# Maximum over keys by VectorE's block transposes, sums of squares by ScalarE's accumulator

## The chip, the core and the metric

The kernel runs on one core of a Trainium2 chip. A core has five engines, each with its own queue that is executed in order: TensorE (PE, matmuls and transposes, with weight loads that overlap), VectorE (DVE), ScalarE (ACT), GpSimd (POOL) and SyncE (SP), which here issues transfers. They wait for each other by semaphores. PE writes only to PSUM, a memory of eight banks of 128 partitions by 512 floats; POOL works on SBUF here.

The metric is the device time of one execution in microseconds, as the median of several. Lower is better.

## What is computed

The reference is a decoder of two layers on 4 sequences of 256 tokens of width 256: self attention, cross attention with a context of 1601 tokens, feed forward, recurrence, a second cross attention, and a mixture of experts. The change lies in the second cross attention, cut here to what matters:

```python
q = (draft_hidden @ Wq.T).reshape(bsz, draft_len, 16, 128)
q = _rms_norm(q, q_norm_w)            # w * x * rsqrt(mean(x*x) + 1e-6)
kv_in = jnp.concatenate([context_hidden, draft_hidden], axis=1)
k = (kv_in @ Wk.T).reshape(bsz, total_len, 4, 128)
v = (kv_in @ Wv.T).reshape(bsz, total_len, 4, 128)
k = _rms_norm(k, k_norm_w)
q = _rope(q, draft_position_ids)
k = _rope(k, full_position_ids)
k = jnp.repeat(k, 4, axis=1); v = jnp.repeat(v, 4, axis=1)
scores = q k^T * SCALE
probs = jax.nn.softmax(scores, axis=-1)
return (probs @ v) @ Wo.T
```

Here the "draft" is the token stream (256 a sequence), so a query sees 256 + 1601 = 1857 keys. There are 16 query heads and 4 key heads; four query heads share a key head.

## The kernel before

The program has two parts. In the first, up to about 540 us, the earlier stages of all sequences run, with preparation of the context's values and some keys in the gaps. The second part is the second cross attention of all sequences, with the experts of finished sequences mixed in; after the last pair the last experts follow.

**Pairs.** The attention is cut into 32 pairs: 4 sequences x 4 key heads x 2, a pair being two query heads of one key head, 512 query columns. The 1857 keys are 15 blocks of 128 (the last has 65 rows); keys lie on the partitions, queries along the free dimension. A pair is run in 8 steps of two blocks. `score` (L1349) multiplies a block of transposed keys with the pair's queries into a PSUM bank `bsc`; ACT copies it to SBUF with the key's norm as a scale (L1350, tile `s`), and DVE folds it with the same scale into a running maximum `acc` over blocks (L1352, L1354). `acc` is 128 x 512: for each query, 128 maxima over 15 keys each.

**Maximum.** `maximum` (L1356) makes of it one number for each query, the same in all partitions. PE transposes the four 128 x 128 squares of `acc` into `tm` (L1361), DVE reduces each row (L1363, `mq`, 128 x 4), and PE transposes the four columns of `mq`, each broadcast along 128, into the bank `bc` (L1367): there each partition holds the 512 maxima.

**Softmax and values.** `exponential` subtracts `bc` from a step's scores (DVE, L1371), takes the exponential (ACT, L1374) and adds the two blocks to a sum on POOL (L1377, L1386). `weigh` (L1395) multiplies values by the exponentials into the bank `po`. `finish` copies `po` (L1401), gets the sums of the queries by `ts` (PE, L1409) and a block transpose (DVE, L1415), and applies the output weights (PE, L1425, then DVE, L1429).

**Queries and keys.** `prep_q` (32 calls, each 128 tokens of four query heads) multiplies tokens with weights into `pq` (L1227); `prep_kv` makes up to four key blocks, two to a bank `pk` (L1278), or takes keys that were kept earlier from memory (`rawk`, sequence 3). Both call `rotate`: ACT squares the bank's numbers into the tile `squares` (L1177), DVE multiplies by the cosine and sine tables (L1178, L1179, tiles `rope` and `ropu`). Then `factor`: POOL adds the halves (L1184), DVE reduces the squares to `ss`, four numbers a partition (L1186), and POOL takes the power -1/2 (L1187, `rnq` for queries, `kn` for keys). The tile `squares` has a 129th column that holds the epsilon. For queries `normed` scales by `rnq` on ACT (L1191), then PE transposes (L1239, `tpq`) and ACT copies to `qT` (L1240); keys are transposed (L1289, `tpk`) and copied to `kT` (L1291).

**PSUM.** In the second part six banks are a ring (`p1`) for all short uses, one is `bc` and one `po`.

**Order.** Step s emits the exponentials of step s - 10, the scores of step s, the pieces put at place 2s, the values of step s - 11, and the pieces put at place 2s + 1. `put` gives a piece its place; with `bank=True` it moves to the next place that no other such piece has. For pair n with last step e, the two pieces of `maximum` stand at 2e + 2 (or the next free place) and 2e + 5. When the program is built, the instructions of all engines are put into a final order for each queue from this emission, so neighbours can change places. `squares` is one tile for all calls.

Of the kernel before, what the change touches and what calls it, by code (L numbers as in the profile page):

```python
# [10 lines left out]
F32 = mybir.dt.float32  # L11
# [4 lines left out]
AF = mybir.ActivationFunctionType  # L16
ALU = mybir.AluOpType
AX = mybir.AxisListType
PSUM = bass.MemoryType.PSUM

P = 128
# [8 lines left out]
NKV, REP, HD1 = 4, 4, 128  # L30
# [86 lines left out]
def decoder_kernel(ctx: ExitStack, tc: tile.TileContext, at, t, out):  # L117
    nc = tc.nc
    V, A, G, T = nc.vector, nc.scalar, nc.gpsimd, nc.tensor
# [6 lines left out]
    fr = ctx.enter_context(tc.tile_pool(name="fr", bufs=1))  # L126
# [11 lines left out]
    def p1(name):  # L138

        ring[0] += 1  # L140
        if psb and ring[0] % 3 == 0:
            return psb[0].tile([P, 512], F32, tag="one", name=name, bufs=2)
        return psa.tile([P, 512], F32, tag="one", name=name, bufs=4)
# [8 lines left out]
    def bank(tag, name):  # L152

        return psb[0].tile([P, 512], F32, tag=tag, name=name) if psb else p1(name)
# [14 lines left out]
    def db(name):  # L169

        return wk.tile([P, 1024], F32, tag="db", name=name, bufs=NDB)

    def sm(shape, tag, name, bufs=2, dt=F32):
        return small.tile(shape, dt, tag=tag, name=name, bufs=bufs)
# [30 lines left out]
    def cc(name):  # L205
        o, n = at[name]
        return cst[:, o : o + n]

    ident = cc("ident")
# [98 lines left out]
    def w512(tag, name):  # L308
        return fr.tile([P, 512], F32, tag=tag, name=name, bufs=2 if tag == "ropu" else NROPE)
# [855 lines left out]
        bt[b]["yT"] = yT.rearrange("p (c t) -> p c t", c=2)  # L1165


    squares = fr.tile([P, 4, HD1 + 1], F32, tag="sqr", name="squares")
    V.memset(squares[:, :, HD1 : HD1 + 1], HD1 * 1e-6)

    def rope_tiles(nm):
        return squares, *(w512(t, f"{t}{nm}").rearrange("p (h d) -> p h d", h=4) for t in ("rope", "ropu"))

    def rotate(src, ctab, stab, sq, r, u):


        A.activation(sq[:, :, 0:HD1], src, AF.Square)  # L1177
        V.tensor_mul(r, src, ctab)  # L1178
        V.tensor_mul(u, src, stab)  # L1179

    def factor(sq, r, u, n, nm, rn):

        r4, u4 = (a[:, 0:n, :].rearrange("p n (h d) -> p n h d", h=2) for a in (r, u))
        G.tensor_tensor(r4, r4, u4[:, :, ::-1, :], ALU.add)  # L1184
        ss = sm([P, 4], "ss4", f"ss{nm}", 4)
        V.tensor_reduce(ss[:, 0:n], sq[:, 0:n, :], AX.X, ALU.add)  # L1186
        G.tensor_tensor(rn, ss[:, 0:n], nhalf[:, 0:n], ALU.pow)  # L1187

    def normed(r, rn, n):
# [3 lines left out]
    def tiles(b, g):  # L1193

        if (b, g) not in gt:
            gt[b, g] = {

                "kT": odd("w3", f"kTb{b}{g}") if g % 2 else wk.tile([P, NKEY], F32, tag="kT", name=f"kTb{b}{g}"),
                "v": (
                    odd("w4", f"vb{b}{g}")[:, 0 : NCH * HD1] if g % 2 else wk.tile([P, NCH * HD1], F32, tag="v", name=f"vb{b}{g}")  # L1200
                ).rearrange("p (c d) -> p c d", c=NCH),
                "kn": sm([P, NCH], f"kn{g % 2}", f"kn{b}{g}", 1),
                "wkv": weight(
                    wk.tile([P, 512], F32, tag="wkv", name=f"wkv{b}{g}", bufs=2), "wkv1", 0, D, g * 256, (g + 1) * 256
                ),
            }
            for i in range(4):
                if (b, i) in kept_values:
                    n, w = units(i)
                    r = min(P, w)  # L1210
                    nc.sync.dma_start(
                        out=gt[b, g]["v"][0:r, 4 * i + 2 : 4 * i + 2 + n, :],
                        in_=kept_values[b, i][:, 0:r, g * HD1 : (g + 1) * HD1].rearrange("c p n -> p c n"),
                    )
        return gt[b, g]
# [30 lines left out]
    def prep_kv(b, g, i):  # L1246

        d, e = bt[b], tiles(b, g)
        nm = f"k{b}{g}{i}"
        n = min(4, NCH - 4 * i)  # L1250
        k0 = max(0, 4 * i - 2)
        w = (4 * i + n - 2 - k0) * P
        done = 0
        if b in kept_keys:
            done = n if i else 2
            raw = db(f"raw{nm}")[:, 0 : done * HD1].rearrange("p (c d) -> p c d", c=done)
            nc.sync.dma_start(
                out=raw, in_=kept_keys[b][k0 : k0 + done, :, g * HD1 : (g + 1) * HD1].rearrange("c p n -> p c n")
            )
        else:  # L1260
            cT = db(f"cT{nm}")[:, 0 : 2 * w].rearrange("p (c n) -> p c n", c=2)
            nc.sync.dma_start(out=cT, in_=t["ctxT"][b][:, k0 * P : k0 * P + w].rearrange("(c p) n -> p c n", p=P))
        sq, r, u = rope_tiles(nm)
        if done:
            o = n - done
            ctab, stab = (a[:, 4 * i + o : 4 * i + n, :] for a in d["k"])
            rotate(raw, ctab, stab, *(a[:, o:n, :] for a in (sq, r, u)))
        for h in range(0, n - done, 2):
            m = min(2, n - h)
            pk = p1(f"p{nm}{h}").rearrange("p (c n) -> p c n", c=2)  # L1270
            there = [k >= 2 and (b, (k - 2) // 4) in kept_values for k in range(4 * i + h, 4 * i + h + m)]
            for q in range(m):
                k = 4 * i + h + q
                w = HD1 if there[q] else 2 * HD1
                for c in range(2):
                    o = (k - 2 - k0) * P
                    src = d["yT"][:, c, k * P : (k + 1) * P] if k < 2 else cT[:, c, o : o + P]
                    T.matmul(pk[:, q, 0:w], lhsT=src, rhs=e["wkv"][:, c, 0:w], start=c == 0, stop=c == 1)  # L1278
            ctab, stab = (a[:, 4 * i + h : 4 * i + h + m, :] for a in d["k"])
            rotate(pk[:, 0:m, 0:HD1], ctab, stab, *(a[:, h : h + m, :] for a in (sq, r, u)))  # L1280
            assert len(set(there)) == 1
            if not there[0]:
                A.copy(e["v"][:, 4 * i + h : 4 * i + h + m, :], pk[:, 0:m, HD1:256])

        factor(sq, r, u, n, nm, e["kn"][:, 4 * i : 4 * i + n])
        yield
        tp = p1(f"tp{nm}")
        for q in range(n):
            T.transpose(tp[:, q * P : (q + 1) * P], r[:, q, :], ident)  # L1289
        w = min(512, NKEY - 512 * i)  # L1290
        A.copy(e["kT"][:, 512 * i : 512 * i + w], tp[:, 0:w])  # L1291

    def before_head(b, g):
# [6 lines left out]
        for i in (1, 2, 3):  # L1300
            gen = prep_kv(b, g, i)
            next(gen)
            yield
            if late:
                run(late)
                yield
            late = gen
# [17 lines left out]
    class Pair:  # L1325
# [30 lines left out]
        def maximum(self):  # L1356

            nm, acc = self.nm, self.acc
            tm = p1(f"tm{nm}")
            for i in range(4):  # L1360
                T.transpose(tm[:, i * P : (i + 1) * P], acc[:, i * P : (i + 1) * P], ident)  # L1361
            mq = sm([P, 4], "mq", f"mq{nm}")
            V.tensor_reduce(mq, tm.rearrange("p (i k) -> p i k", i=4), AX.X, ALU.max)  # L1363
            yield
            self.bc = bank("bc", f"bc{nm}")
            for i in range(4):
                T.transpose(self.bc[:, i * P : (i + 1) * P], mq[:, i : i + 1].to_broadcast([P, P]), ident)  # L1367

        def exponential(self, c):
            n, w, s = self.rows[c], self.wide[c], self.s[c]  # L1370
# [77 lines left out]
    def put(place, gen, last=False, bank=False):  # L1448
        while bank and place in taken:
            place += 1  # L1450
        if bank:
            taken.add(place)
        places.setdefault(place, []).append((gen, last))
        return place

    def loader(b, g):
        load_wo(b, g)
        yield

    def tokens(b):  # L1460
        normed_tokens(b)
        yield
        bt[b]["xh"] = bt[b]["centred"]()
        yield
        token_features(b)
        yield

    for n, pair in enumerate(pairs):
        e = NPAIR * n + NPAIR - 1
        gen = pair.maximum()  # L1470
        put(2 * e + 2, gen, bank=True)
        put(2 * e + 5, gen, True)
        e += DW
        gen = pair.finish()
        put(2 * e + 1, gen)
        if not pair.final:
            put(2 * e + 4, gen, bank=True)
        put(2 * e + 7, gen, pair.final, bank=True)
        if not pair.final:
            put(2 * e + 10, gen, True, bank=True)  # L1480
    for k, (b, g) in enumerate(heads):
        base = 32 * (k - 1)
        if k:
            if g == 0:
                gen = angles(b)
                for i in range(9):
                    put(base - 81 + 6 * i, gen, i == 8)
                gen = tokens(b)
                for i, o in enumerate((-8, -6, -3)):
                    put(base + o, gen, i == 2, i == 2)  # L1490
                for o, n in ((-5, "q"), (-3, "q"), (7, "k"), (11, "k")):
                    gen = tables(b, n) if o in (-5, 7) else gen
                    put(base + o, gen, o in (-3, 11))
            for f, when in ((prep_q, QA), (prep_kv, KA)):
                for i, o in enumerate(when):
                    gen = f(b, g, i)
# [4 lines left out]
        gen = loader(b, g)  # L1501
        put(base + 60, gen, True)
    for b in range(B - 1):
        gen = experts(b)
# [81 lines left out]
    gen = experts(B - 1)  # L1586
# [71 lines left out]
```

## Time and profile before

| | us |
|---|---|
| median of 3 runs (1750.13 to 1754.91) | 1750.22 |
| span of the profiled execution | 1749.1 |
| PE busy in 560 to 1690 us (1130 us) | 1112.0 |
| DVE busy there | 902.6 |
| ACT busy there | 682.7 |
| POOL busy there | 751.3 |
| one pair, from one last score to the next (mean of 31) | 37.1 |

How to read the lines further down. The page's first line gives for each engine the busy time, its share of the span and its instructions; the granted clock of PE was 1.00 over 560 to 1690 us. The "chain that ended last" is the sequence of work followed back from the last instruction, at each step to what released it; its shares say which engine the end waited for. A line of a group has line number, engine, operation, tiles, shape and count, then total busy time in us and mean in ns, then the idle time of the engine just ahead of them and what ended it. A line of the chain in order of time has start, length, engine, line, tile and count; a line of the timeline has start, length, engine, line, operation, tiles, shape, count, and the idle time ahead in brackets.

### The profile page before, as it was taken

How to read it: one execution, taken by the hardware profiler on the slowest of the kernel's cores; microseconds unless marked ns; L12 is line 12 of the kernel's file. 1: busy time of each engine (PE TensorE's matmuls, PEld its weight loads, DVE VectorE, ACT ScalarE, POOL GpSimd, SP SyncE). 2: the span in 40 equal slices, each digit the busy share in tenths (PEclk: the TensorE clock that was granted, in tenths of full speed). 3: DMA queues.
4: the chain of work that ended last, by engine and by line, in shares of the span. 5: the costliest groups of instructions: out<-in, count | busy, mean ns of one | idle time of the engine just before them, and what ended most of it. 6: DMA issues, size and time to landing. Idle time of an engine off the chain costs nothing.

```text
span 1749.1 us, 20626 instructions
## 1 busy us (share of the span) xinstructions
PE 1691.1 (97%) x6636; PEld 970.2 (55%) x6636; DVE 1302.7 (74%) x2428; ACT 998.2 (57%) x1741; POOL 877.0 (50%) x719
## 2 busy tenths in 40 slices
PE   7989989999999999999999999999999999999998
PEld 4555668765555454554555555555555555455546
DVE  5662575788658787787878879787877878888776
ACT  2457653555456566566565646656564655656551
POOL 2210023311016667677666656765666777576651
PEclk9999999999999999999999999999999999999999
DMA  6321234213231021111212121120212112011102
GB/s 226 119 95 55 79 98 136 71 57 104 94 115 43 33 89 28 61 35 54 78 38 64 47 76 52 55 83 31 76 52 73 46 45 91 9 56 49 43 0 67
DMA packets 113138, 119.10 MB, mean 68 GB/s; under 512 B 9968, under 2 KB 86660, under 8 KB 113032
## 3 DMA queue, kind: packets, MB, share of 16 engines
q1 hardware_dynamic: 111736, 116.25, 21.4%
q10 hardware_dynamic: 1296, 1.54, 0.3%
q8 instruction: 53, 0.87, 0.2%
q14 instruction: 53, 0.43, 0.1%
HBM read 100.20 MB, written 17.57 MB: 67 GB/s over the span
## 4 chain that ended last, share of the span: by engine, by line
PE 65%; DVE 12%; POOL 9%; ACT 9%; issue 4%; DMA 1%; POOLq 0%; ACTq 0%; DVEq 0%
PE bpo L1395 16%; PE bsc L1349 16%; PE pk L1278 5%; POOL sum L1386 5%; PE mph L1041 2%; PE bpw L1425 2%; PE vah L348 2%; ACT s L1374 2%; ACT s L1350 2%; DVE acc L1354 1%; PE xpo L728 1%; DVE s L1371 1%; PE pq L1227 1%; POOL ropeq L1184 1%; PE sc L564 1%
## 5 line engine op out<-in xcount | busy, mean ns | idle before, releaser
L1386 POOL TENSOR_TENSOR sum<-sum,s 128x512 f32<-128x512 f32 (+1 forms) x411 | 537.5, 1308 | 84.0 <-ACT s L1374 58.9
L1349 PE MATMUL bsc<-qTb,kTb 128*128 128x512 f32 (+1 forms) x960 | 458.4, 597 | 6.6 <-ACT kTb L1291 6.3
L1395 PE MATMUL bpo<-s,vb 128*128 128x512 f32 (+1 forms) x960 | 458.7, 596 | 0.4 <-ACT s L1374 0.4
L1350 ACT ACTIVATE s<-bsc,kn 128x512 f32<-128x512 f32 (+1 forms) x480 | 317.4, 684 | 210.9 <-PE bsc L1349 193.7
L1354 DVE SCALAR_TENSOR_TENSOR acc<-bsc,kn,acc 128x512 f32<-128x512 f32 x448 | 332.4, 742 | 88.0 <-ACT s L1350 75.0
L1371 DVE TENSOR_TENSOR s<-s,bc 128x1024 f32<-128x1024 f32 (+1 forms) x256 | 289.0, 1140 | 14.8 <-PE bc L1367 14.8
L1374 ACT ACTIVATE s<-s 128x1024 f32<-128x1024 f32 (+1 forms) x256 | 256.6, 1006 | 52.0 <-DVE s L1371 50.5
L1349 PEld LDWEIGHTS bsc<-qTb,kTb 128*128 128x128 f32 (+1 forms) x960 | 173.9, 187 | 191.1 <-issue 135.7
L1395 PEld LDWEIGHTS bpo<-s,vb 128*128 128x128 f32 (+1 forms) x960 | 169.7, 190 | 141.5 <-issue 137.4
L1184 POOL TENSOR_TENSOR ropek<-ropek,ropuk 128x512 f32<-128x512 f32 (+1 forms) x64 | 78.3, 1224 | 123.8 <-DVE ropuk L1179 119.4
L1377 POOL TENSOR_TENSOR sum<-s 128x512 f32<-128x512 f32 x32 | 40.9, 1279 | 195.9 <-ACT s L1374 195.9
L1191 ACT ACTIVATE ropeq<-ropeq,rnq 128x128 f32<-128x128 f32 x128 | 41.2, 390 | 109.7 <-POOL rnq L1187 106.0
L348 PE MATMUL vah<-wv,vcT 128*128 128x512 f32 (+1 forms) x156 | 77.9, 636 | 5.6 <-DMA vcT<-in_ctxT 3.6
L1278 PEld LDWEIGHTS pk<-wkv,cTk 128*128 128x128 f32 x624 | 76.3, 192 | 8.3 <-issue 4.8
L1278 PE MATMUL pk<-wkv,cTk 128*128 128x128 f32 x624 | 77.4, 275 | 0.0
L1187 POOL TENSOR_TENSOR kn<-ssk,nhalf 128x4 f32<-128x4 f32 (+1 forms) x64 | 66.2, 1035 | 17.5 <-DVE ssk L1186 17.5
L1425 PEld LDWEIGHTS bpw<-wo,aT 128*128 128x128 f32 x256 | 48.5, 190 | 34.8 <-issue 22.0
L269 POOL TENSOR_TENSOR rsr_xa<-rse_xa,nhalf 128x2 f32<-128x2 f32 x4 | 3.4, 854 | 126.0 <-DVE rse_xa L267 126.0
L1425 PE MATMUL bpw<-wo,aT 128*128 128x256 f32 x256 | 65.6, 379 | 0.3 <-ACT aT L1401 0.3
L1352 DVE TENSOR_SCALAR acc<-bsc,kn 128x512 f32<-128x512 f32 x32 | 24.0, 750 | 56.3 <-ACT s L1350 56.3
L1184 POOL TENSOR_TENSOR ropeq<-ropeq,ropuq 128x512 f32<-128x512 f32 x32 | 43.9, 1371 | 40.2 <-PE bsc L1349 17.8
L351 ACT COPY vst<-vah 128x512 f32<-128x512 f32 (+1 forms) x52 | 30.3, 592 | 58.4 <-PE vah L348 20.6
(505 smaller groups left out, 2584.5 us busy)
## 6 DMA issues: line engine op xcount, KB each, us to landing
v<-vst SPq DMA_DIRECT2D x48, 256.0 KB
vb<-v SPq DMA_DIRECT2D x48, 256.0 KB
cTk<-in_ctxT SPq DMA_DIRECT2D x24, 512.0 KB
wq<-in_wq SPq DMA_DIRECT2D x16, 512.0 KB
wo<-in_wo SPq DMA_DIRECT2D x16, 512.0 KB
wi<-in_wi SPq DMA_DIRECT2D x32, 256.0 KB
vcT<-in_ctxT SPq DMA_DIRECT2D x12, 512.0 KB
xcT<-in_ctxT SPq DMA_DIRECT2D x12, 512.0 KB
```

Of the source, the lines that this page charges most:

```text
L348: T.matmul(pv[0:r, :], lhsT=cT[:, c, k * P : k * P + r], rhs=wv[c], start=c == 0, stop=c == 1)
L1184: G.tensor_tensor(r4, r4, u4[:, :, ::-1, :], ALU.add)
L1187: G.tensor_tensor(rn, ss[:, 0:n], nhalf[:, 0:n], ALU.pow)
L1278: T.matmul(pk[:, q, 0:w], lhsT=src, rhs=e["wkv"][:, c, 0:w], start=c == 0, stop=c == 1)
L1349: T.matmul(pc[0:n, :], lhsT=e["kT"][:, k * P : k * P + n], rhs=q, start=True, stop=True)
L1350: A.activation(s[0:n, i, :], pc[0:n, :], AF.Copy, scale=e["kn"][0:n, k : k + 1])
L1354: V.scalar_tensor_tensor(self.acc[0:n, :], pc[0:n, :], e["kn"][0:n, k : k + 1], self.acc[0:n, :], ALU.mult, ALU.max)
L1371: V.tensor_tensor(s[0:n, 0:w, :], s[0:n, 0:w, :], self.bc[0:n, None, :].to_broadcast([n, w, 512]), ALU.subtract)
L1374: A.activation(s[0:n, 0:w, :], s[0:n, 0:w, :], AF.Exp)
L1386: G.tensor_tensor(self.sum[0:n, :], self.sum[0:n, :], s[0:n, i, :], ALU.add)
L1395: T.matmul(self.po, lhsT=e["v"][0:n, k, :], rhs=self.s[c][0:n, i, :], start=k == 0, stop=k == NCH - 1)
L1425: T.matmul(pw[:, j * 256 : j * 256 + 256], lhsT=aT[:, o : o + P], rhs=e["wo"][:, self.h + h, :], start=True, stop=True)
```

## The change

Two edits, and two places for the pieces of `maximum`.

*Maximum.* DVE transposes `acc` in blocks of 32 x 32 straight into a bank `tr`, so that within each of 4 x 16 blocks keys and queries change places, and reduces over each block's 32 columns to `top`, 128 x 16: for each query, four partial maxima in the four groups of 32 partitions. One PE transpose brings `top` to 16 x 128 (`tm`); DVE reduces over the four groups (`mq`, 16 x 32) and repeats the result four times (`mqf`, 16 x 128); one PE transpose brings this to 128 x 16 (`tq`); and a block transpose by DVE of `tq`, each column repeated 32 times, writes `bc`.

*Sums of squares.* ACT squares each 128 x 128 block by itself and adds up its rows in the instruction's accumulator output, into `ss`; `squares` keeps only the elements, which nobody reads. DVE adds the epsilon to `ss` in place of the reduction.

*Places.* `maximum` has three pieces: at 2e, at 2e + 2 and at 2e + 4, the last two at places free of other pieces that take a bank.

```diff
-    squares = fr.tile([P, 4, HD1 + 1], F32, tag="sqr", name="squares")
-    V.memset(squares[:, :, HD1 : HD1 + 1], HD1 * 1e-6)
+    squares = fr.tile([P, HD1], F32, tag="sqr", name="squares")
...
-    def rotate(src, ctab, stab, sq, r, u):
-        A.activation(sq[:, :, 0:HD1], src, AF.Square)
+    def rotate(src, ctab, stab, ss, r, u):
+        for i in range(ss.shape[1]):
+            A.activation(squares, src[:, i, :], AF.Square, accum_out=ss[:, i : i + 1])
         V.tensor_mul(r, src, ctab)
         V.tensor_mul(u, src, stab)
...
-        ss = sm([P, 4], "ss4", f"ss{nm}", 4)
-        V.tensor_reduce(ss[:, 0:n], sq[:, 0:n, :], AX.X, ALU.add)
+        V.tensor_scalar(ss[:, 0:n], ss[:, 0:n], HD1 * 1e-6, None, ALU.add)
         G.tensor_tensor(rn, ss[:, 0:n], nhalf[:, 0:n], ALU.pow)
...
         def maximum(self):
             nm, acc = self.nm, self.acc
+            tr = p1(f"tr{nm}")
+            V.transpose(tr, acc)
+            top = sm([P, 16], "top", f"top{nm}")
+            V.tensor_reduce(top, tr.rearrange("p (b k) -> p b k", k=32), AX.X, ALU.max)
+            yield
             tm = p1(f"tm{nm}")
-            for i in range(4):
-                T.transpose(tm[:, i * P : (i + 1) * P], acc[:, i * P : (i + 1) * P], ident)
-            mq = sm([P, 4], "mq", f"mq{nm}")
-            V.tensor_reduce(mq, tm.rearrange("p (i k) -> p i k", i=4), AX.X, ALU.max)
-            yield
+            T.transpose(tm[0:16, 0:P], top, ident)
+            mq = sm([16, 32], "mq", f"mq{nm}")
+            V.tensor_reduce(mq, tm[0:16, 0:P].rearrange("b (a i) -> b i a", a=4), AX.X, ALU.max)
+            mf = sm([16, 4, 32], "mqf", f"mqf{nm}")
+            V.tensor_copy(mf, mq[:, None, :].to_broadcast([16, 4, 32]))
+            yield
+            tq = p1(f"tq{nm}")
+            T.transpose(tq[:, 0:16], mf.rearrange("b a i -> b (a i)"), ident[0:16, 0:16])
             self.bc = bank("bc", f"bc{nm}")
-            for i in range(4):
-                T.transpose(self.bc[:, i * P : (i + 1) * P], mq[:, i : i + 1].to_broadcast([P, P]), ident)
+            V.transpose(self.bc.rearrange("p (b k) -> p b k", k=32), tq[:, 0:16, None].to_broadcast([P, 16, 32]))
...
         gen = pair.maximum()
+        put(2 * e, gen)
         put(2 * e + 2, gen, bank=True)
-        put(2 * e + 5, gen, True)
+        put(2 * e + 4, gen, True, bank=True)
```

More of the change, by code (lines that the diff above doesn't have):

```diff
@@ L1165, in token_features, with factor @@
         bt[b]["yT"] = yT.rearrange("p (c t) -> p c t", c=2)
-    squares = fr.tile([P, 4, HD1 + 1], F32, tag="sqr", name="squares")
-    V.memset(squares[:, :, HD1 : HD1 + 1], HD1 * 1e-6)
+    squares = fr.tile([P, HD1], F32, tag="sqr", name="squares")
     def rope_tiles(nm):
-        return squares, *(w512(t, f"{t}{nm}").rearrange("p (h d) -> p h d", h=4) for t in ("rope", "ropu"))
-    def rotate(src, ctab, stab, sq, r, u):
-        A.activation(sq[:, :, 0:HD1], src, AF.Square)
+        ss = sm([P, 4], "ss4", f"ss{nm}", 4)
+        return ss, *(w512(t, f"{t}{nm}").rearrange("p (h d) -> p h d", h=4) for t in ("rope", "ropu"))
+    def rotate(src, ctab, stab, ss, r, u):
+        for i in range(ss.shape[1]):
+            A.activation(squares, src[:, i, :], AF.Square, accum_out=ss[:, i : i + 1])
         V.tensor_mul(r, src, ctab)
         V.tensor_mul(u, src, stab)
-    def factor(sq, r, u, n, nm, rn):
+    def factor(ss, r, u, n, nm, rn):
         r4, u4 = (a[:, 0:n, :].rearrange("p n (h d) -> p n h d", h=2) for a in (r, u))
         G.tensor_tensor(r4, r4, u4[:, :, ::-1, :], ALU.add)
-        ss = sm([P, 4], "ss4", f"ss{nm}", 4)
-        V.tensor_reduce(ss[:, 0:n], sq[:, 0:n, :], AX.X, ALU.add)
+        V.tensor_scalar(ss[:, 0:n], ss[:, 0:n], HD1 * 1e-6, None, ALU.add)
         G.tensor_tensor(rn, ss[:, 0:n], nhalf[:, 0:n], ALU.pow)
@@ L1266, in prep_kv @@
             ctab, stab = (a[:, 4 * i + o : 4 * i + n, :] for a in d["k"])
-            rotate(raw, ctab, stab, *(a[:, o:n, :] for a in (sq, r, u)))
+            rotate(raw, ctab, stab, *(a[:, o:n] for a in (sq, r, u)))
         for h in range(0, n - done, 2):
@@ L1279, in prep_kv @@
             ctab, stab = (a[:, 4 * i + h : 4 * i + h + m, :] for a in d["k"])
-            rotate(pk[:, 0:m, 0:HD1], ctab, stab, *(a[:, h : h + m, :] for a in (sq, r, u)))
+            rotate(pk[:, 0:m, 0:HD1], ctab, stab, *(a[:, h : h + m] for a in (sq, r, u)))
             assert len(set(there)) == 1
```

## The prediction

> **What bounds the kernel now.** I read the page's busy shares first, then the chain that ended last, then the chain in order of time inside the second cross attention, and last the groups of the lines the change touches.
>
> ```profile
> PE 1691.1 (97%) x6636; PEld 970.2 (55%) x6636; DVE 1302.7 (74%) x2428; ACT 998.2 (57%) x1741; POOL 877.0 (50%) x719
> PE 65%; DVE 12%; POOL 9%; ACT 9%; issue 4%; DMA 1%; POOLq 0%; ACTq 0%; DVEq 0%
> ```
>
> TensorE (PE) is busy 97% of the span and carries 65% of the chain. But a busy PE need not work at its pace, so the pace is taken from the chain, which lists matmuls by the distance from one to the next:
>
> ```profile
> 847.70 1.72 PE bsc L1349 x4
> 849.42 1.78 PE pk L1278 x16
> 852.92 0.86 PE bpw L1425 x4
> 865.54 0.44 PE tm L1361 x4
> 872.05 0.44 PE bc L1367 x4
> 905.31 0.79 PE pl L993 x8
> 919.15 0.36 PE ts L1409 x8
> ```
>
> A 512-wide pass costs 1.72/4 = 0.43 us, a 256-wide one 0.215, a pk 0.111, a transpose 0.11, a ts 0.045, a pl 0.10. Between 560 and 1690 us the groups of PE count 1925 passes of 512, 604 of 256, 548 pk, 604 transposes, 240 ts and 24 pl: 828 + 130 + 61 + 66 + 11 + 2 = 1098 us of work in 1130 us. PE is 97% full by pace too. In this stage DVE is busy 77 to 84% of each 100 us, ACT 56 to 64%, POOL 60 to 72% (busy time by stretches).
>
> ```profile
> L1191 ACT ACTIVATE ropeq<-ropeq,rnq 128x128 f32<-128x128 f32 x128 | 41.2, 390 | 109.7 <-POOL rnq L1187 106.0 <-POOL ropeq L1184 3.7
> L1363 DVE TENSOR_REDUCE mq<-tm 128x4 f32<-128x512 f32 x32 | 21.8, 681 | 2.3 <-PE tm L1361 2.2
> L1367 PE MATMUL bc<-cst,mq 128*128 128x128 f32 x128 | 20.0, 280 | 7.2 <-DVE mq L1363 7.2
> L1415 DVE STREAM_TRANSPOSE sq<-ts 128x128 f32<-128x128 f32 x32 | 9.8, 305 | 1.4 <-PE ts L1409 1.4
> L1186 DVE TENSOR_REDUCE ssk<-squares 128x4 f32<-128x516 f32 x48 | 32.5, 676 | 3.8 <-ACT squares L1177 3.8
> L1177 ACT ACTIVATE squares<-pk 128x256 f32<-128x256 f32 x88 | 33.3, 387 | 17.5 <-PE pk L1278 15.7 <-ACT kTb L1291 1.7
> L1177 ACT ACTIVATE squares<-pk 128x128 f32<-128x128 f32 x12 | 3.3, 277 | 0.8
> ```
>
> The 32 missing microseconds of PE come mostly from where ACT, in order, stands 106 us in all (31 times, 3.4 us each) before L1191, for POOL's rnq; keys and scores behind it are late then.
>
> **Part 1, PE.** Per pair eight transposes go and two come. Removed: 32 x 8 x 0.11 = 28.2 us. Added: tm, 128 wide, 0.11; tq, 16 wide, between a ts (0.045) and a transpose (0.11), nearest to pl's 8 columns at 0.10: 32 x 0.21 = 6.7. Net -21.5 us (-23.2 to -21.1). On a PE that is 97% full this counts in full if the others keep up.
>
> **Part 2, DVE, the maximum.** Removed: one reduction, 0.68. Added: two block transposes of 128x512, a 512-wide reduction, a 16x128 reduction and a 16x128 copy. No 128x512 transpose is in the trace. Bounds: 0.305 (the 128x128 one) and 4 x 0.305 = 1.22; I take 0.305 plus what 384 more columns cost a tensor_tensor (0.684 at 512, 0.280 at 128): 0.71. The wide reduction is 0.68 by L1363; the small one 0.28 (0.17 to 0.42, by the 128x16 and 128x256 reductions: 0.16 and 0.41); the copy 0.20 by a 13x128 conversion (0.17 to 0.28). Sum 0.71 + 0.68 + 0.28 + 0.20 + 0.71 = 2.58, so +1.90 a pair, +61 us in all (+30 to +100).
>
> The row first: four PE transposes take 0.44 us of the full engine, and the 128x128 block transpose 0.305 of one that has 20% left. The Trainium skill ("VectorE: DVE Perf Modes", Rules for kernel authors) says the opposite of this edit: a 128x128 transpose belongs on TensorE, DVE does only 32x32 blocks, and chained DVE operations should be few. By the rule the edit is a loss of the +61 us; by the rows it is a gain of 21.5, as DVE is not what fills.
>
> **Part 3, DVE, the sums of squares.** 96 reductions go: 32.5 + 8.7 + 21.7 = 62.9 us. 96 additions on 128x4 come, 0.17 each by the 128x4 tensor_scalar of L267: 16.3. So DVE in all: 61 - 63 + 16 = +14 us (-17 to +54), 1% of the span. At DVE's 12% of the chain: +1.7 us.
>
> **Part 4, ACT.** 148 squares (64.4 us over their six forms) become 368 of 128x128, each with an accumulator output. The plain one takes 0.277. No accumulator output is in the trace. Below: 368 x 0.277 - 64.4 = +37. Above: a second small instruction each, as long as the smallest ACTIVATE of the trace (128x2, 0.204): +113. The nearest row is L1191, a 128x128 with one small second operand, 0.390: 143.5 - 64.4 = +79 us, which I take. It lies in ACT's idle time (40% of the stage); at ACT's 9% of the chain it costs 7 us, nothing if hidden, 79 if the cover is gone. What stands behind a longer square on ACT are the copies s<-bsc that free PSUM banks, and on DVE the product L1178, which waits for the square of the same bank.
>
> The skill ("VectorE: DVE Perf Modes", Two Vector instructions with no wait between them) counts a Vector operation with an accumulator output as two instructions, the operation and a read. It speaks of VectorE; if ACT does likewise, the upper end, +113, is the right one, 3 us more on the path. No run here shows it.
>
> **Part 5, the new waits.** Before, PE's queue held tm, which needs acc, and bc, which needs mq; only a few bc waited, 7.2 us in all.
>
> ```profile
> 858.89 0.75 DVE L1354 SCALAR_TENSOR_TENSOR acc<-bsc,kn,acc 65x512 f32<-65x512 f32 x1 [1.82 <-ACT s L1350]
> 865.38 0.60 PE L1361 MATMUL tm<-cst,acc 128*128 128x128 f32 x4
> ```
>
> Here acc ends at 859.6 and tm starts 5.7 us later. Over all pairs acc ends 1.7 to 4.8 us after the last score's matmul. Now tm needs acc, block transpose and reduction in DVE's queue, and behind tm PE's queue holds bpo and the next pair's bsc. In the order in which the changed program stands, PE has 5 to 8 us of work at the paces above between the last bsc and tm; DVE has, after acc's 1.7 to 2.5, 0.7 to 2.3 us of other work, 0.71, up to 0.7 and 0.68: 3.8 to 6.9. Second pairs of a key head have margin, first pairs none: 16 x 0.25 = 4 us. From tm to tq PE mostly has 2.6 us of work, DVE 0.28 + 0.68 + 0.20 and the latencies: just enough. I take +4 us; bounds -7 (bc's old waits go, none come) and +32 (64 waits of half a microsecond). DVE's wait for bc (14.8 us at L1371) goes, since bc is now its own. Three PSUM banks of the ring instead of one are taken for 1 to 2 us each per pair, within the same bounds.
>
> **Without cost:** additions of places only move pieces within the built order. On SP one load of kept keys (rawk) now stands behind two stores of out; before, they left at 1470.51 and 1470.96, side by side: nothing. POOL keeps its work; rnq now always stands directly behind ropeq, where before 9 of 32 had a sum between, or stood before it, which is at most a gain of 9 x 1.3 us of waiting that is off PE. The last pair: bc was 6.9 us behind the last score's matmul, now about 6.3: nothing.
>
> **Sum.** -21.5 + 1.7 + 7 + 4 = -9 us against the profiled span of 1749.1; the median of the runs, 1750.2, is 1.1 above that span, which I take as what lies around it: 1740.1 + 1.1 = 1741 us.
>
> **Rivals.**
> *All of it arrives.* ACT's and DVE's additions lie in idle time and bc's waits of 7 us go in part: -21.5 - 3: 1726 us. For it: PE is full by pace, ACT 40% idle. Against: POOL, DVE and ACT together hold 30% of the chain, so not every freed microsecond of PE is one of the end.
> *The chain moves to the preparation of the queries.* PE reaches each of the 32 spots at L1191 earlier and waits there: POOL's sum, ropeq and rnq (1.3 + 1.2 + 1.0 us) set the pace. If each takes back 0.65 us, 21 us are gone: 1750 us. For it: the 106 us of ACT waiting. Against: PE has some 14 to 17 us of work between pq and tpq.
> *Slower: DVE stands behind the squares.* L1178 and L1179 are in DVE's queue and wait for four squares where they waited for one. By 0.390 a square: queries 4 x 0.390 - 0.594 = 0.97, x32 = 31 us; keys 2 x 0.390 - 0.387 = 0.39, x88 = 35 us; 66 us in which DVE stands, and acc, which frees the score banks of PE, stands behind. DVE's 903 busy us of these 1130 become 903 + 14 + 66 = 983, 87%. If half reaches PE, -21.5 + 1.7 + 4 + 33 = +17: 1767 us. It decides from a quarter (16 us) on: then the sum is zero. For it: L1178 already waited 25.7 us for the queries' squares. Against: the build's order fills the gap with other work of DVE.
> That the change does not do what it says is ruled out: the changed program has 192 matmuls fewer and 220 ACTIVATEs more.
>
> **Numbers.** Forecast 0.45 (own range 1732 to 1750), all arrives 0.17, back to nothing 0.16, slower 0.22. A measurement of this kernel tells 0.3%, 5 us, from no change, so faster is below 1745. Faster: 0.17 and four fifths of the forecast, 0.54; same: 0.21; slower: 0.25. The range runs from the full arrival, 1725, to short of the slower rival, 1761.
>
> **What would show it.** tm and tq together 32 x 0.21 us of PE, L1395 and L1349 unchanged; DVE's block transposes at 0.7; ACT squares at 0.28 to 0.48 with or without a second instruction behind; idle of PE before tm and tq under 10 us. It is wrong if block transposes take over 1.2 us, if PE stands over 20 us before tm and tq, or if DVE's wait for squares rises above 60 us.

## The result and the profile after

The changed kernel takes 1771.59 us (median of 4 runs, 1770.46 to 1772.84), the kernel before 1751.69 us (4 runs, 1750.13 to 1754.91). The ratio is 1.0113, 95% interval 1.0100 to 1.0125: 20 us slower, where 9 us faster was forecast. The profiled execution spans 1770.8 us.

The page after, its first line and the shares of the chain that ended last:

```profile
PE 1684.8 (95%) x6444; PEld 945.7 (53%) x6444; DVE 1336.5 (75%) x2555; ACT 1055.1 (60%) x2329; POOL 872.6 (49%) x719
PE 59%; ACT 14%; DVE 14%; POOL 7%; issue 5%; DMA 1%; POOLq 0%; ACTq 0%; DVEq 0%; SPq 0%
```

No other engine became full. PE has 192 matmuls less, but its share of the chain fell from 65% to 59%, and ACT's rose from 9% to 14%: PE stands more. Where, the groups after show (busy time and mean, then the idle time of the engine ahead of them):

```profile
L1191 ACT ACTIVATE ropeq<-ropeq,rnq 128x128 f32<-128x128 f32 x128 | 43.8, 392 | 111.4 <-POOL rnq L1187 111.4
L1365 PE MATMUL tm<-cst,top 128*16 128x128 f32 x32 | 8.7, 273 | 9.5 <-DVE top L1362 7.7 <-ACT ropeq L1191 1.9
L1372 PE MATMUL tq<-cst,mqf 16*128 16x16 f32 x32 | 7.2, 227 | 19.1 <-DVE mqf L1369 18.2 <-ACT s L1350 0.9
L1360 DVE STREAM_TRANSPOSE tr<-acc 128x512 f32<-128x512 f32 x32 | 22.8, 713 | 0.1
L1374 DVE STREAM_TRANSPOSE bc<-tq 128x512 f32<-128x512 f32 x32 | 23.0, 719 | 0.8 <-PE tq L1372 0.8
L1186 DVE TENSOR_SCALAR ssk<-ssk 128x4 f32<-128x4 f32 x48 | 22.9, 476 | 3.2 <-ACT squares L1178 3.2
L1178 ACT ACTIVATE squares<-pk 128x128 f32<-128x128 f32 x188 | 52.4, 279 | 30.9 <-PE pk L1278 27.4
L1178 ACT ACTIVATION_READ_ACCUMULATOR squares<-pk 128x1 f32 x188 | 37.7, 201 | 0.0
L1179 DVE TENSOR_TENSOR ropek<-pk,ctabk 128x256 f32<-128x256 f32 x88 | 36.8, 418 | 16.2 <-ACT squares L1178 13.5 <-PE pk L1278 1.7 <-DMA k<-kst 0.4
L1349 PE MATMUL bsc<-qTb,kTb 128*128 128x512 f32 x896 | 430.7, 602 | 14.1 <-ACT kTb L1291 10.2 <-DVE acc L1354 1.9 <-DVE ssq L1186 1.4
```

PE stands 9.5 us before tm and 19.1 us before tq, 28.6 us in all; the prediction called itself wrong from 20 us on. Before, the two groups in these places (tm and bc) had 0.8 and 7.2 us. The last line shows a second place where PE waits: its scores stand 10.2 us for ACT's copy of the transposed keys, `kTb` (6.3 us before).

How such a wait comes about, in the timeline of after, first PE, then DVE (start, length, engine, line, operation; the wait stands in brackets). Of the 32 pairs it is the one with the longest way on DVE from the start of tm to the end of mqf, 6.8 us; the mean is 2.9.

```profile
1075.11 0.28 PE L1365 MATMUL tm<-cst,top 128*16 128x128 f32 x1 [1.15 <-DVE top L1362]
1075.23 1.02 PE L1402 MATMUL bpo<-s,vb 128*128 128x512 f32 x2
1076.09 1.88 PE L1349 MATMUL bsc<-qTb,kTb 128*128 128x512 f32 x4
1077.81 1.02 PE L1402 MATMUL bpo<-s,vb 128*128 128x512 f32 x2
1081.93 0.23 PE L1372 MATMUL tq<-cst,mqf 16*128 16x16 f32 x1 [3.10 <-DVE mqf L1369]
1082.09 1.12 PE L1402 MATMUL bpo<-s,vb 128*128 128x512 f32 x2
```

```profile
1077.59 0.42 DVE L1047 SCALAR_TENSOR_TENSOR it<-it,mph 128x256 f32<-128x256 f32 x1 [2.53 <-ACT it L1046]
1078.75 0.75 DVE L1352 TENSOR_SCALAR acc<-bsc,kn 128x512 f32<-128x512 f32 x1 [0.74 <-ACT s L1350]
1079.41 0.41 DVE L1048 TENSOR_TENSOR it<-it,mph 128x256 f32<-128x256 f32 x1
1079.74 0.74 DVE L1354 SCALAR_TENSOR_TENSOR acc<-bsc,kn,acc 128x512 f32<-128x512 f32 x1
1080.40 0.27 DVE L1367 TENSOR_REDUCE mq<-tm 16x32 f32<-16x128 f32 x1
1080.60 1.14 DVE L1126 SCALAR_TENSOR_TENSOR ang<-sn,ang 128x960 f32<-128x960 f32 x1
1081.67 0.21 DVE L1369 COPY mqf<-mq 16x128 f32<-16x128 f32 x1
```

tm is done at 1075.4. mq needs nothing more, but stands in DVE's queue behind work that waits for ACT (2.53 and 0.74 us), and comes 5.0 us later; between mq and mqf stands another operation, of 1.14 us. PE has 3.4 us of work between tm and tq, so it waits 3.1 us.

### The profile page after: what moved, and what is told of

The parts are those of the page before. It is cut to its first block, busy times and chain, and to the rows that moved or that the text cites. A ratio compares the mean times of both kernels' runs of the same rounds, so it can differ in the third digit from the quotient of the medians.

```text
span 1770.8 us, 20974 instructions
## 1 busy us (share of the span) xinstructions
PE 1684.8 (95%) x6444; PEld 945.7 (53%) x6444; DVE 1336.5 (75%) x2555; ACT 1055.1 (60%) x2329; POOL 872.6 (49%) x719
## 4 chain that ended last, share of the span: by engine, by line
PE 59%; ACT 14%; DVE 14%; POOL 7%; issue 5%; DMA 1%; POOLq 0%; ACTq 0%; DVEq 0%; SPq 0%
PE bpo L1402 15%; PE bsc L1349 15%; PE pk L1278 5%; ACT s L1350 3%; ACT s L1381 3%; PE vah L348 3%; DVE acc L1354 2%; POOL sum L1393 2%; PE mph L1041 2%; ACT ropeq L1191 2%; PE pq L1227 2%; PE bpw L1432 2%; POOL rnq L1187 2%; PE xpo L728 1%; DVE s L1378 1%
## 5 line engine op out<-in xcount | busy, mean ns | idle before, releaser
L1349 PE MATMUL bsc<-qTb,kTb 128*128 128x512 f32 (+1 forms) x960 | 463.2, 601 | 14.1 <-ACT kTb L1291 10.2
L1402 PE MATMUL bpo<-s,vb 128*128 128x512 f32 (+1 forms) x960 | 463.5, 598 | 0.0
L1191 ACT ACTIVATE ropeq<-ropeq,rnq 128x128 f32<-128x128 f32 x128 | 43.8, 392 | 111.4 <-POOL rnq L1187 111.4
L1187 POOL TENSOR_TENSOR kn<-ssk,nhalf 128x4 f32<-128x4 f32 (+1 forms) x64 | 65.1, 1019 | 16.3 <-DVE ssk L1186 13.5
L1178 ACT ACTIVATE squares<-pk 128x128 f32<-128x128 f32 x188 | 52.4, 279 | 30.9 <-PE pk L1278 27.4
```

Of the source, the lines that this page charges most:

```text
L1349: T.matmul(pc[0:n, :], lhsT=e["kT"][:, k * P : k * P + n], rhs=q, start=True, stop=True)
L1402: T.matmul(self.po, lhsT=e["v"][0:n, k, :], rhs=self.s[c][0:n, i, :], start=k == 0, stop=k == NCH - 1)
```

## The experiments

Times are medians; "before" is the kernel before on the same chip. Unless said, kernels start from after. Outside every range that was expected for them fell e3, e5, h1 and h2 by 1 us or less, and f2, f3, g1, g2, g4 and h4 by more (f2 and h4 on the fast side).

| kernel | us | before | ratio, 95% interval |
|---|---|---|---|
| e1_max_only | 1763.07 | 1753.77 | 1.0049 (1.0033 to 1.0065) |
| e2_squares_only | 1752.53 | 1753.77 | 0.9992 (0.9983 to 1.0002) |
| e3_split_only | 1757.14 | 1753.77 | 1.0018 (1.0008 to 1.0027) |
| e5_sq_no_eps | 1743.32 | 1753.77 | 0.9936 (0.9921 to 0.9951) |
| f1_no_copy | 1758.49 | 1753.77 | 1.0036 (1.0023 to 1.0048) |
| f2_late | 1747.75 | 1753.77 | 0.9968 (0.9956 to 0.9979) |
| f3_pe_free | 1756.40 | 1753.77 | 1.0018 (1.0009 to 1.0027) |
| f4_no_eps | 1750.16 | 1753.77 | 0.9978 (0.9969 to 0.9987) |
| g1_eps_reduce | 1776.78 | 1753.01 | 1.0143 (1.0127 to 1.0158) |
| g2_best | 1751.10 | 1753.01 | 0.9993 (0.9983 to 1.0004) |
| g3_max_late | 1748.67 | 1753.01 | 0.9980 (0.9970 to 0.9989) |
| g4_late_pe_kept | 1765.89 | 1753.01 | 1.0079 (1.0064 to 1.0094) |
| h1_power_first | 1757.88 | 1753.63 | 1.0029 (1.0019 to 1.0038) |
| h2_power_late | 1743.80 | 1753.63 | 0.9946 (0.9932 to 0.9960) |
| h3_second_late | 1778.65 | 1753.63 | 1.0143 (1.0128 to 1.0157) |
| h4_third_late | 1745.16 | 1753.63 | 0.9955 (0.9940 to 0.9970) |
| i1_power_third_late | 1741.36 | 1751.51 | 0.9947 (0.9934 to 0.9959) |
| i2_before_early | 1780.38 | 1751.51 | 1.0170 (1.0154 to 1.0185) |

### Each edit alone

e1 is before with the new `maximum` and its places (mq and mqf lie in `acc`, for room). e2 is before with the squares by the accumulator. e3 is before with only this:

```diff
-        A.activation(sq[:, :, 0:HD1], src, AF.Square)
+        for i in range(sq.shape[1]):
+            A.activation(sq[:, i, 0:HD1], src[:, i, :], AF.Square)
```

> Only the maximum by block transposes and its three places; sums of squares as before. mq and mqf lie inside acc, to have room for them. If the loss is ACT's and DVE's for the squares (theory S), this arm keeps the gain of TensorE: 21.5 us less work, some of it given back before tm and tq, so 1730 to 1748. If the loss is TensorE standing before tm and tq (theory M: 28.6 us idle there in the changed kernel, 8.0 before bc and tm in the old one), this arm is slower than before: 1760 to 1775. If both have a part, about 1750.

> Only the sums of squares by ACT's accumulator; the maximum as before. Theory S: 1772 to 1795, since TensorE's saving is missing and the squares cost all that is lost. Theory M: 1750 to 1756. Both: about 1765 to 1772.

> Kernel before, with each square cut into squares of 128 columns, but no accumulator output and the reduction on DVE as before. ACT has 37 us more, without the 368 reads of the accumulator (74 us). If the reads make the loss of the squares, this stays within 1750 to 1757; if the cut into single blocks, and DVE's wait for the last of them, makes it, this is as slow as the arm with the accumulator.

The maximum alone loses 9 us, the squares alone nothing (-1.2), cutting the squares 3.4. The whole loses 20, more than the sum of its parts. DVE waiting for squares is not it: e2 has all the squares of after at no loss, and DVE waits for squares 13.5 us before L1179's 128x256 products in after, not 66.

### Making PE independent of DVE, or the chain between shorter

f1 leaves out the copy mqf; PE makes the four repeats itself. f3 lets both transposes read the identity, so that bc doesn't hold the maximum.

```diff
-            mf = sm([16, 4, 32], "mqf", f"mqf{nm}")
-            V.tensor_copy(mf, mq[:, None, :].to_broadcast([16, 4, 32]))
...
-            T.transpose(tq[:, 0:16], mf.rearrange("b a i -> b (a i)"), ident[0:16, 0:16])
+            for a in range(4):
+                T.matmul(tq[32 * a : 32 * a + 32, 0:16], lhsT=mq, rhs=ident[0:16, 0:16], start=True, stop=True)
```

```diff
-            T.transpose(tm[0:16, 0:P], top, ident)
+            T.transpose(tm[0:16, 0:P], ident[:, 0:16], ident)
...
-            T.transpose(tq[:, 0:16], mf.rearrange("b a i -> b (a i)"), ident[0:16, 0:16])
+            T.transpose(tq[:, 0:16], ident[0:16, :], ident[0:16, 0:16])
```

> The changed kernel without the copy mqf: four products of 16 columns, each to 32 partitions of tq, put the maxima four times instead. The copy takes 204 ns at best and up to 1378 in the changed kernel, mean 311, and TensorE stands 18.2 us before tq for it. If the copy is what holds tq (theory C), 1755 to 1763; if tq waits for DVE's queue as a whole (theory Q: mq and the acc products ahead), at most 5 us faster than the changed kernel, 1766 to 1773.

> The changed kernel with both TensorE transposes of the maximum reading the constant identity instead of top and mqf, so that they wait for no DVE work of the maximum. The subtracted maximum is then not the maximum: it leaves out that dependence, all instructions stay. Theory Q: 1738 to 1752, as the standing before tm and tq is gone. Theory D: 1762 to 1772.

Without the copy 13 us come back, and PE before tq stands 9.9 instead of 19.1 us. With PE free of DVE 15 us come back; PE before tm and tq stands 5.1 us, but the weight loads of its scores still wait 43.1 us for kTb. So the waits of tm and tq together are worth about 15 us, and they are not all.

### The places

```diff
-        put(2 * e + 2, gen, bank=True)
-        put(2 * e + 4, gen, True, bank=True)
+        put(2 * e + 3, gen, bank=True)
+        put(2 * e + 5, gen, True)
```

f2 is after with these places; g3 is e1 with them. h3 has the first of the two lines alone, h4 the second alone. g4 is f2 with six transposes of the identity more per pair (192 in all, 21.1 us at 0.11), which nobody reads. i2 is before, with nothing else than its last piece put where after has it:

```diff
-        put(2 * e + 5, gen, True)
+        put(2 * e + 4, gen, True, bank=True)
```

> The changed kernel with the second piece of the maximum at 2e + 3 instead of 2e + 2 and the third at 2e + 5, as before the change, instead of 2e + 4. Theory Q: later places leave TensorE more work ahead of tm and tq, its standing there falls from 26 to under 10 us and the time to 1750 to 1760. If the loss is the work on DVE itself (theory D: what DVE does more delays acc and the scores, wherever TensorE stands), 1766 to 1775, and the lost time of TensorE goes to other lines.

> Only the maximum, sums of squares as before, with the places 2e, 2e + 3, 2e + 5. With the places of the change this arm was at 1763. Theory Q (cushion ahead of tm and tq): 1740 to 1750. If the later places help only together with the squares, 1757 to 1765.

> The kernel with later places, with six more PE transposes of the constant identity per pair beside tm and tq, which nobody reads: TensorE has the work of the kernel before again, 32 x 6 x 0.11 = 21 us more. If a microsecond of TensorE's work is a microsecond of the time, as the forecast took it, 1767 to 1771. If TensorE is held by the others, less: 1749 to 1758.

> After, with the second piece of maximum (tm) at 2e + 3 instead of 2e + 2, the third as it is at 2e + 4 or the next free place. If the wait of tm is what costs: 1750 to 1757 us. If it is the wait of tq behind tm (19.1 us of PE standing against 9.5): no better than 1765 us, since tq then follows tm closer or at the same distance.

> After, with the third piece of maximum (tq) at 2e + 5, the second as it is at 2e + 2. If the wait of tq costs the most: 1752 to 1760 us, PE before tq under 5 us. If it is the wait of tm and what stands behind it: 1765 to 1772 us.

> Before, with its last piece of maximum (the transposes into bc) at 2e + 4 or the next free place, instead of 2e + 5, and nothing else. If the distance between two pieces of PE is what decides, whatever DVE does between them: slower than before by over 10 us, PE standing before bc for well over 7.2 us. If only the changed chain (three steps of DVE between tm and tq) needs the distance: within 5 us of before.

h4 and i2 settle it. Moving the third piece alone turns +20 us into -8.5. Moving it in before, with none of the changed work, costs 29 us. Between these four kernels place and work hardly mix: the changed work is worth -8.5 us at the old place (h4 against before) and -8.8 at the new one (after against i2), or -7.9 and -9.8 by the ratios. With the maximum as the only change the two places cost less, 14 us (e1 against g3). The second piece's place is no help (the intervals of f2 and h4 overlap), and moved late with the third piece early it costs 5 to 7 us more (h3).

i2's miss matters: I had expected that, if the distance decides, the wait before bc would grow well beyond 7.2 us. It grew to 14.8 only, a fraction of the 29. The first lines of the pages, i2's and then h4's:

```profile
PE 1703.1 (96%) x6636; PEld 972.8 (55%) x6636; DVE 1302.9 (73%) x2428; ACT 1001.9 (56%) x1741; POOL 876.0 (49%) x719
PE 1682.1 (96%) x6444; PEld 948.1 (54%) x6444; DVE 1337.8 (77%) x2555; ACT 1058.7 (61%) x2329; POOL 870.9 (50%) x719
```

The profiled span of i2 (1778.8 us) is 29.7 us longer than that of before. PE's idle time in it is 17.7 us longer (75.7 against 58.0) and its busy time 12.0, for the same 6636 matmuls. Those 12 us match a lower clock. In the second part of i2 the trace has the granted clock at 0.50 in seven stretches of 3.4 or 6.8 us, 30.8 us in all, each during or just behind a stand of PE of 1.9 to 6.0 us; before has two, 6.8 us in all. At half the clock that loses 15.4 us against 3.4. It is no accident of one execution: the mean granted clock was 0.987 or 0.988 in all four runs of i2, 0.993 to 0.996 in those of before. In e1 and g1 such stretches lose 10.2 and 13.7 us, in after and g3 5.1 each. After against h4 has no such part (5.1 us lost against 6.8). The profiled span of after is 25.1 us longer than h4's, and PE's idle time has 22.4 of them (86.0 against 63.6): 14.8 before tq and 5.8 before the scores.

In the list of waits (sum, times, longest), i2's and then h4's:

```profile
ACT ropeq L1191 <- POOL rnq L1187: 108.9, 31, 8.1
PEld bsc L1349 <- ACT kTb L1291: 35.4, 46, 4.0
PEld bc L1367 <- DVE mq L1363: 19.3, 7, 6.8
PE bc L1367 <- DVE mq L1363: 14.8, 4, 6.0
PE bsc L1349 <- ACT kTb L1291: 10.7, 6, 3.6
```

```profile
ACT ropeq L1191 <- POOL rnq L1187: 85.3, 27, 6.6
PEld bsc L1349 <- ACT kTb L1291: 19.7, 25, 2.3
PEld tq L1372 <- DVE mqf L1369: 10.7, 8, 3.9
PE bsc L1349 <- ACT kTb L1291: 4.5, 4, 2.0
PE tq L1372 <- DVE mqf L1369: 4.3, 4, 3.1
```

The weight loads of the scores wait for kTb 35.4 us in i2, 38.2 in after, 19.7 in h4 (20.4 in before). These waits alone do not give the time: f3 and h1, 15 and 14 us faster than after, have 43.1 and 35.2. The place lengthens them, it seems, because of `bank=True`: the third piece now claims 2e + 4 as its own, and what else wanted this place moves on. Worked out from `put`, 15 of the 60 key transpositions and 9 pieces of experts move one place back in after, none in h4. PE's queue as built shows it; lines with - are h4's, with + after's:

```
-L1289 Matmult tpk<-cst,ropek 128x128 x4
-L1278 Matmult pk<-wkv,cTk 128x128 x4
-L1278 Matmult pk<-wkv,cTk 128x128 x2
+L1372 Matmult tq<-cst,mqf 128x16
+L1278 Matmult pk<-wkv,cTk 128x128 x4
+L1278 Matmult pk<-wkv,cTk 128x128 x2
 L1402 Matmult bpo<-s,vb 128x512 x2
-L1372 Matmult tq<-cst,mqf 128x16
+L1289 Matmult tpk<-cst,ropek 128x128 x4
```

At this spot the keys are transposed six pk and two bpo later, and tq comes that much earlier. With tq the exponentials and POOL's sums come earlier too: ahead of a head's first ropeq, POOL's built queue has 6 sums where h4 has 3 in 9 of 14 heads, and once 11 where h4 has 4. This last spot, in the chain of after in order of time (start, length, what):

```profile
818.46 1.27 POOL sum L1393
819.80 0.11 POOL sum L1393
819.92 1.11 issue
821.03 1.27 POOL ropeq L1185
822.30 0.99 POOL rnq L1187
823.31 1.28 ACT ropeq L1191 x4
824.58 0.57 ACT s L1350
825.16 0.52 ACT s L1381
825.68 0.57 ACT s L1350
826.25 0.32 ACT kTb L1291
826.61 3.78 PE bsc L1349 x4
```

POOL works off its sums (1.35 us each), then ropeq and rnq; ACT's scaling waits for rnq, the key copy kTb stands behind the scaling, and PE's scores wait for kTb: 4.35 us of idle PE ahead of 826.61 in the timeline of after, 3.57 us at the like spot of i2, none in h4. The four scores behind that gap take 3.78 us, where four took 1.72 in the chain of before: the granted clock is 0.50 from 824.4 on, for 6.8 us. No run put the third piece early without claiming its place, so what part of the 26 to 29 us each of the three has (tq close to tm, the late key transpositions, the sums ahead of ropeq) stays open. f3, which frees tm as well as tq, puts the waits of both at about 15 us.

g4 against f2 measures what a freed microsecond of PE is worth: 21.1 us of transposes cost 18.1, or 0.86 each (19.5 us and 0.92 by the ratios). g3 shows the maximum alone at the late places: from +9.3 to -4.3 us.

### The epsilon

In e5 (from e2) and f4 (from after) the addition of the epsilon is left out. g1 adds it in another form, by a reduction over pairs of a sum and a constant. h1 keeps the addition, but puts it right behind the squares in `rotate`, and puts POOL's power ahead of POOL's own addition:

```diff
-        V.tensor_scalar(ss[:, 0:n], ss[:, 0:n], HD1 * 1e-6, None, ALU.add)
+        V.tensor_reduce(se[:, 0:n], ss[:, 0:n, :], AX.X, ALU.add)
```

```diff
             A.activation(squares, src[:, i, :], AF.Square, accum_out=ss[:, i : i + 1])
+        V.tensor_scalar(ss, ss, HD1 * 1e-6, None, ALU.add)
...
-        G.tensor_tensor(r4, r4, u4[:, :, ::-1, :], ALU.add)
-        V.tensor_scalar(ss[:, 0:n], ss[:, 0:n], HD1 * 1e-6, None, ALU.add)
         G.tensor_tensor(rn, ss[:, 0:n], nhalf[:, 0:n], ALU.pow)
+        G.tensor_tensor(r4, r4, u4[:, :, ::-1, :], ALU.add)
```

> The arm with only the sums of squares, without DVE's addition of the epsilon (the epsilon is left out). In the changed kernel these 96 additions take 0.14 to 1.27 us each, 41.7 us in all where 16 were forecast, and they lie near POOL's additions. If DVE's standing in them is a part of the loss, this arm is 10 to 25 us faster than the one with the addition; if only ACT counts, they are the same within 4 us.

> The changed kernel without DVE's addition of the epsilon (left out). With the maximum as before this addition cost 9.2 us. If costs add up, 1760 to 1765; if DVE's fullness makes them worse together (the two parts alone gave +9.3 and -1.2 where the whole gives +20), 1750 to 1759.

> The changed kernel with the epsilon added by a reduction over pairs of numbers (the sum and a constant that stands beside it) instead of the tensor_scalar. As many DVE instructions as in the changed kernel, of about 0.16 us by the small reductions of L1006. In the changed kernel the tensor_scalar that began at 931.79 ended at 932.67, where an addition of POOL ended too. If the tensor_scalar stands until POOL's running instruction ends and the reduction does not (theory P), L1186 takes 0.13 to 0.20 us throughout and the time is that without the addition, 1748 to 1756. If it is the additional instruction in the chain that costs (theory N), 1765 to 1773.

> After, with the epsilon added on DVE directly behind the squares and the power on POOL (L1187) placed ahead of POOL's addition (L1184) where it can be: in the built order the queries' power stands ahead in 32 of 32 (0 of 32 in after), the keys' in 57 of 64 (7 of 64). The DVE additions stay, 128 of them or so. If the loss by the epsilon is the place of the power on POOL: 1748 to 1757 us, and ACT stands about 85 us ahead of L1191 instead of 111. If it is the additional step on DVE: 1766 to 1774 us, the standing of ACT unchanged or without effect.

Leaving the addition out gains 9 us on e2 and 21 on after. Its time on DVE is not why: g1's form takes a third of it and is no faster than after (5 us slower, with 8.6 us more lost to the lower clock).

```profile
L1191 DVE TENSOR_REDUCE ssk<-sums 128x4 f32<-128x8 f32 x48 | 7.2, 149 | 3.5 <-ACT squares L1182 3.3 <-POOL kn L1192 0.2
```

What fits all of them is the order on POOL: without the addition the built queue has the queries' power ahead of ropeq in 32 of 32 cases, with it in none (before has it in one). h1 keeps every addition, has the power ahead in 32 of 32, and gains 14 us on after. Its timing missed the expected range by 0.9 us. ACT now waits before the scaling for POOL's addition, no longer for the power:

```profile
L1191 ACT ACTIVATE ropeq<-ropeq,rnq 128x128 f32<-128x128 f32 x128 | 43.6, 391 | 73.3 <-POOL ropeq L1187 73.3
```

73.3 us, against 111.4 in after: 1.2 us less for each of 32 scalings. h1 also moves the addition ahead of DVE's products; the two moves weren't tried apart.

### Together

g2 is f2 with f1's and g1's edits; h2 is h1 with f2's places; i1 is h1 with h4's place.

> The changed kernel with all three repairs: the places 2e, 2e + 3, 2e + 5, no copy mqf (four small products), the epsilon by a reduction. Alone they gave -24, -13 and, by leaving the addition out, -21 us against the changed kernel. If each takes away a different part of the loss, down to the forecast's gain of TensorE, 1728 to 1738; if all three relieve the same cushion ahead of TensorE, about the best one alone, 1741 to 1748.

> The kernel with the power ahead of the addition, and the places of maximum 2e, 2e + 3 and 2e + 5. If the place of the power and the places of maximum relieve different waits: 1733 to 1743 us, under both kernels. If both only give PE the same reserve, 1745 to 1750 us, as the late places alone (0.9968 of before).

> After, with the power ahead of POOL's addition (as in the kernel with the power first) and the third piece of maximum at 2e + 5, the second at 2e + 2. If the two gains have different causes they add in part: 1733 to 1741 us. If what is left after the late third piece is little, as with all three pieces late (1743.8 against 1747.75 without the power): 1741 to 1745 us.

g2 was a miss: on top of f2 the edits of f1 and g1 together lose 3 us, and which of them does isn't separated. i1 is faster than both kernels: 1741.36 us, 0.9947 of before. The power first is worth 14 us in after, but once the third piece is late only 3.8 by the medians and 1.4 by the ratios, whose intervals overlap (i1 against h4; h2 against f2 is like it, 4 us by the medians). So the two gains don't add: with the place given back little of the other is left.

## Why the prediction was wrong

The failed step is the one in "Without cost": "additions of places only move pieces within the built order". It priced the place at nothing, without a reason; it costs 26.4 us by medians (after against h4) and 29 us without any of the changed work (i2). I had taken the third piece's move from 2e + 5 to 2e + 4 as a detail and had not followed what the claim of a place displaces. Part 5 is the term of the sum that this made wrong: it took +4 us for the new waits, from 2.6 us of PE's work between tm and tq against 0.28 + 0.68 + 0.20 us on DVE. PE's standing before tm and tq grew from 8.0 to 28.6 us. DVE's queue holds work that itself waits for ACT, as the timeline shows at its worst, and from the start of tm to the end of mqf the 32 pairs take 2.9 us in the mean, in after as in h4. PE's work in that gap is 3.3 us in the mean in after and 5.6 in h4. At the old place PE stands 9.6 + 4.3 = 13.9 us before tm and tq, 5.9 more than before, so there the +4 was near. Part 5's upper bound, +32, would have held the 20.6; the value taken didn't.

The rest, step by step. With the place given back (h4) the kernel is 8.5 us faster than before, against the -9 of the sum. That is in part luck: alone, the maximum with both pieces late is worth -4.3 us (g3) and the squares -1.2 (e2), where Parts 1 to 5 make some -10 and +1 of them.

- *Part 1, PE*, right in mechanism: g4 against f2. tq goes by 0.16 us (1081.93 to 1082.09), not 0.10: 2 us in all. That a microsecond of PE counts in full was a little too much (0.86).
- *Part 2*, right: block transposes 0.71 and 0.72 us, and 22.8 + 21.7 + 8.6 + 10.0 + 23.0 - 21.8 = +64 us against +61. The Trainium skill ("VectorE: DVE Perf Modes", Rules for kernel authors) sends a whole 128x128 transpose to TensorE and calls DVE fastest for 32x32 blocks within a bank. This edit works in such blocks, so the rule is not its opposite, as the prediction had it. Here the transposes taken from PE, the full engine, are worth having (g4 is 18.1 us slower than f2, and h4 beats before).
- *Part 3*, mis-sized: the additions of the epsilon took 22.9 + 14.4 + 4.4 = 41.7 us, not 16.3. Besides, with them POOL's power stands behind ropeq. "Without cost" saw that order, which before has too, and not that the other one is worth 14 us in after (h1).
- *Part 4*, within its bounds: ACT's busy time rose by 57 us, not 79. Each accumulator output is a second instruction of 0.19 to 0.20 us, 37.7 + 26.1 + 9.9 = 73.7 us over 368 of them, in part beneath the squares. All records of the squares together grew by 113 us, the upper bound of Part 4. The skill's sentence on two instructions (same page, Two Vector instructions with no wait between them) is about VectorE; ACT's rows show the like. On the path the squares, with what they change on DVE, cost nothing (e2).
- The rival *Slower: DVE stands behind the squares* came near in time (1767) by a mechanism that didn't happen: DVE waited less for squares than before (13.5 + 2.1 us for the products of L1179, against 30.7 for those of L1178 before). *The chain moves to the preparation of the queries* named the right neighbourhood: POOL's ropeq and rnq, with ACT behind, set the pace at the spot shown above. *All of it arrives* (-24 us) was reached by no run; the nearest are e5, without the epsilon, with -10.4 and i1 with -10.2.
- The reading that PE's 32 missing us in before come mostly from ACT's standing is not shown by the lines of before: PE itself waited 6.3 us there before the scores for kTb, less than the 7.2 before bc.

## What to carry to other kernels

A place in a hand-made order is a resource: price a move by what it displaces on every queue, not only by the moved piece, and move the place alone in the old kernel before crediting or blaming the work that came with it. Where a chain goes from the full engine to another and back, count what stands in the other engine's queue and what that work waits for, not only the chain's own durations. And where a small step stands can matter more than its time, if it decides the order of a third engine's queue. When a wait does not explain a loss, compare the busy time of the same instructions and the granted clock.

## Unexpected on the hardware

A DVE addition on 128x4 numbers, 0.14 us at best, took up to 1.27 us, 0.48 in the mean for the keys. The timelines of after, DVE then POOL, show why:

```profile
931.79 0.88 DVE L1186 TENSOR_SCALAR ssk<-ssk 128x4 f32<-128x4 f32 x1
```

```profile
925.95 10.79 POOL L1393 TENSOR_TENSOR sum<-sum,s 128x512 f32<-128x512 f32 x8 [1.29 <-ACT s L1381]
```

The fifth of the eight sums ends at 932.64, DVE's addition at 932.67. So it is throughout after: 49 of the 96 additions began while POOL ran an addition of its own, and each of them ended 0.02 to 0.03 us behind that one, after 0.19 to 1.27 us. The other 47, three of them beside POOL's power, took 0.14 to 0.17 us. The same sum as a reduction over pairs took 0.12 to 0.16 us in all 96 cases, though 48 began beside an addition of POOL (g1); the time of the kernel did not show it.
